# Hyperbolic loops of a four-layer graph network: the 65th coordinate's sums taken once per two row blocks

## The chip, the cores and the metric

The kernel runs on one core of one Trainium2 chip. The metric is device time of a run in microseconds (us). TensorE is PE in the profile, VectorE DVE, ScalarE ACT, GpSimd POOL; SP's queue issues nearly all DMAs.

## What is computed

Four layers run over 3327 nodes with 64 features each, padded to 3328 = 26 blocks of 128; every layer adds to x what it computes from a normalised x and the 0/1 adjacency matrix. Layers 0 and 3 are the hyperbolic ones:

```python
h = relu(layernorm(x))
x_tan = logmap0(h)
adj_att = sigmoid(left + right.T) * adj         # left, right: x_tan times a vector
x_local = logmap(h[:, None, :], h[None, :, :])  # hyperbolic log between every two nodes
support = einsum('ij,ijd->id', adj_att, x_local)
x = x + proj(expmap(h, support))
```

Layer 1 sums neighbours with weights that halve along a row, layer 2 is a signed attention with two gated cells; both need only the adjacency matrix and x. Layer 3 is layer 0 with other constants and a curvature.

## The kernel before, in words

**The form of a hyperbolic layer.** The log between two nodes is a factor, which depends on an inner product of 65 coordinates, times a combination of both points. So a layer needs a weight for each pair of nodes (sigmoid times adjacency times an arctangent of the inner product plus a constant) and then the sum over nodes of weight times the node's 65 coordinates. Coordinates 1 to 64 are in Xr, the 65th (x0) in X0.

**Tiles.** `hyperbolic_series` holds the 3328 output nodes in two halves of 13 blocks; its chunks take 4, 3, 3 and 3 blocks of each half, so that one tile is 128 source nodes by 2 x 512 or 2 x 384 output nodes. For each chunk it goes over the 26 row blocks of source nodes: K = 104 tiles, numbered k, in the order chunk, then row block b. Two row blocks that follow each other (2j and 2j + 1) are a pair.

**One tile's way.**
- `load` (L368) brings the adjacency tile by a DMA of SP's queue, in layer 0 only; layer 3 finds it in SBUF as fp8 masks, which layer 1 made.
- `sigmoid` (L568) writes `sig` on ScalarE; L570 multiplies the adjacency into it on GpSimd.
- `products` (L581, L582) makes the inner products on TensorE, two fp16 matmuls for each half, into a PSUM slot.
- `angle` (L587) takes the arctangent in place on ScalarE.
- `weights` (L591) adds PC and multiplies by `sig` on VectorE, the result into `sig`; then the slot is free.
- `sums` (L600) multiplies Xr of the row block with `sig`, 64 output rows for each half, in fp32. After every second row block L608 does the same for the 65th coordinate: X0 is 32 columns wide, only its first is not zero, and the four operands (two row blocks, two halves) stand side by side in the array's four column groups, 32 output rows each. So a pair has one such group of matmuls, and `to_m2` (L639) adds the rows of the two row blocks later.

Four PSUM slots serve all this. One is the accumulator of the running chunk; three go round for products.

**The order.** The program in the loops is written by hand: under `manual_schedule` ScalarE, VectorE, TensorE and GpSimd run their instructions as written, each in its order. Step j issues sums of tiles 2j - 2 and 2j - 1, products of 2j + 3 and 2j + 4, weights of 2j and 2j + 1, arctangents of 2j + 2 and 2j + 3, sigmoids of 2j + 3 and 2j + 4. At the end of a chunk `out_of` (L618, ScalarE) takes the sums out, `back` (L627) transposes them, and `to_m`, `to_m2` (L633 to L643, VectorE, with copies on ScalarE) reduce them. SP's DMAs stand in an order that the tile framework chooses from when their buffers are free. In layer 0 GpSimd also makes `diag` (L560), two operations for each chunk.

**Ahead of the loops** the points are normalised and split in fp16 parts: Xp and Xe hold the parts that TensorE transposes, LT a row vector of `left`, which a DMA (L534) writes to memory so that later chunks read it back as `leftB` (L388). The first tile's sigmoid stands behind the last preparation on VectorE (L537). **After layer 0** come some 15 us of small VectorE operations, and then layer 1, whose loads (L1289, 832 KB each, seven buffers) and masks (L1317) need nothing of layer 0's result.

Of the kernel before, what the change touches and what calls it, by code (L numbers as in the profile page):

```python
# [19 lines left out]
P = 128  # L20
T = 26
NP = T * P
D = 64
# [6 lines left out]
PA, PB, PC, PF = 0.8235022297, 1.4, 1.7857925668, 1.1972493614  # L30
# [16 lines left out]
def tile_gnn4(ctx: ExitStack, tc: tile.TileContext, x, adjT, att0, b0, w1, bias1, w_gat, a_gat,  # L47
# [4 lines left out]
    V, G, A, PE = nc.vector, nc.gpsimd, nc.scalar, nc.tensor  # L52
# [268 lines left out]
    def hyperbolic_series(r, params, ok, masks=None, done=None):  # L321
# [17 lines left out]
        W = 512  # L339
        with ExitStack() as st:  # L340
            pers = st.enter_context(tc.tile_pool(name="hs", bufs=1))
            Xr = pers.tile([P, T, D], F32, name="Xr")
            X0 = pers.tile([P, T, 32], F32, name="X0")
            x2 = pers.tile([P, T], F32, name="x2")
            ia = pers.tile([P, T], F32, name="ia")
            XT = pers.tile([P, NP], F16, name="XT")

            XE = pers.tile([KE + 9, NP], F16, name="XE")
            Xp = pers.tile([P, T, 2 * D + 9], F16, name="Xp")
            hi, lo, F = Xp[:, :, :D], Xp[:, :, D:2 * D], Xp[:, :, 2 * D:]  # L350
            LT = pers.tile([T, P], F32, name="LT")
            right = pers.tile([P, T], F32, name="right")
            M = pers.tile([P, T, D], F32, name="M")
            M0, hm, mm = [pers.tile([P, T], F32, name=n) for n in ("M0", "hm", "mm")]
# [4 lines left out]
            px = st.enter_context(tc.tile_pool(name="hsx", bufs=2))  # L359
            small = {n: pers.tile([P, T], F32, name=n) for n in ("rr", "k", "kb", "bx", "bk", "bh")}  # L360
            adjs = {}
            tiles = [(c, b) for c in chunks for b in range(T)]
            K = len(tiles)

            def load(k):
                c, b = tiles[k]
                adjs[k] = px.tile([P, 2, W], F32, name="adj", bufs=4)[:, :, :c[1] * P]
                nc.sync.dma_start(adjs[k], halves(adjT[b * P:(b + 1) * P, :], c))  # L368

            XC, XF, leftB = {}, {}, {}  # L370
# [1 line left out]
            def halves(t, c):  # L372

                return t.rearrange("p (o i) -> p o i", o=2)[:, :, c[0] * P:(c[0] + c[1]) * P]
# [14 lines left out]
                                                        ap=[[0, P], [HT * P, 2], [1, n]]))  # L389

            if masks is None:
                for k in range(4):
                    load(k)
            with tc.tile_pool(name="hsp", bufs=1) as tp, tc.tile_pool(name="hsps", bufs=2, space=PSUM) as ps, \
                    tc.manual_schedule(engines={mybir.EngineType.Activation, mybir.EngineType.DVE,
                                                mybir.EngineType.PE, mybir.EngineType.Pool}):
                H, R, sq, sr = [tp.tile([P, T, D], F32, name=n) for n in ("H", "R", "sq", "sr")]
                Xe = tp.tile([P, T, KE + 9], F16, name="Xe")
                E, Fe = Xe[:, :, D:KE], Xe[:, :, KE:]
                G.memset(X0, 0.0)  # L400
                G.memset(E[:, :, 6:], SX)
# [4 lines left out]
                def new(name):  # L406
                    return tp.tile([P, T], F32, name=name)
# [40 lines left out]
                x0, x0s, rest, z, lr, left, good = [new(n) for n in ("x0", "x0s", "rest", "z", "lr2", "left", "good")]  # L448
# [83 lines left out]
                PE.transpose(junk[:T, :P], left, ident)  # L532
                V.tensor_copy(LT, junk[:T, :P])
                nc.sync.dma_start(left_row, LT)  # L534
                V.tensor_copy(X0[:, :, 0], x0)
                V.scalar_tensor_tensor(good, x2, X2_MIN, nodes, op0=OP.is_ge, op1=OP.mult)
                V.reduce_sum(ok, good, axis=AX.X)  # L537

# [4 lines left out]
            with tc.tile_pool(name="hsw", bufs=2) as wk, tc.tile_pool(name="hsps", bufs=1, space=PSUM) as ps, \  # L543
                    tc.manual_schedule(engines={mybir.EngineType.Activation, mybir.EngineType.DVE,
                                                mybir.EngineType.PE, mybir.EngineType.Pool}):
                acc, sigs, Ls, later = {}, {}, {}, {}
                slots = [ps.tile([P, 2, W], F32, name=f"slot{k}") for k in range(4)]
                made = [0]

# [14 lines left out]
                def sigmoid(k):  # L564

                    c, b = tiles[k]
                    sig = sigs[k] = new("sig", c, bufs=7)
                    A.activation(sig, leftB[c], AF.Sigmoid, bias=right[:, b:b + 1])  # L568
                    adj = adjs.pop(k) if masks is None else halves(masks[b // 2][:, b % 2, :], c)
                    G.tensor_tensor(sig, adj, sig, op=OP.mult)  # L570

                def products(to):

# [10 lines left out]
                def angle(k):  # L584

                    L = Ls[k][:, :, :tiles[k][0][1] * P]
                    A.activation(L, L, AF.Arctan, scale=PA / SX ** 2)  # L587

                def weights(k):
                    slot, sig = Ls.pop(k), sigs[k]  # L590
                    V.scalar_tensor_tensor(sig, slot[:, :, :tiles[k][0][1] * P], PC, sig, op0=OP.add, op1=OP.mult)  # L591
                    slots.append(slot)

                def sums(k):
                    c, b = tiles[k]
                    n = c[1] * P
                    if b == 0:
                        acc[c] = slots.pop(0)
                    for o in range(2):
                        PE.matmul(acc[c][o * D:(o + 1) * D, 0, :n], Xr[:, b, :], sigs[k][:, o, :],  # L600
                                  start=b == 0, stop=b == T - 1)
                    if b % 2 == 1:

                        for i in range(2):
                            w = sigs.pop(k - 1 + i)
                            for o in range(2):
                                q = 32 * (2 * i + o)
                                PE.matmul(acc[c][q:q + 32, 1, :n], X0[:, b - 1 + i, :], w[:, o, :],  # L608
                                          start=b == 1, stop=b == T - 1, tile_position=(0, q))
                    if b == T - 1:  # L610
                        a = new("sum", c, bufs=1)
                        j = (k + 1) // 2
                        later[j, 1] = lambda: out_of(c, a, 0)
                        later[j + 1, 0] = lambda: out_of(c, a, 1)
                        later[j + 2, 0] = lambda: back(j + 2, c, a)

                def out_of(c, a, o):
                    A.activation(a[:, o, :], acc[c][:, o, :c[1] * P], AF.Copy)  # L618
                    if o == 1:
                        slots.append(acc.pop(c))  # L620
# [8 lines left out]

                def to_m(j, c, slot):  # L630
                    pm = slot[:, 0, :c[1] * P].rearrange("p (t o d) -> p o t d", o=2, d=D)
                    prod = wk.tile([P, 2, 2, 4, D], F32, name="prod", bufs=1)[:, :, :, :c[1], :]
                    V.tensor_mul(prod[:, 0], by_tiles(Xr, c), pm)  # L633
                    A.activation(prod[:, 1], pm, AF.Square)
                    later[j + 1, 0] = lambda: to_m2(j + 1, c, slot, pm, prod)
# [12 lines left out]

                sigmoid(0)
                for j in range(-1, K // 2 + 5):  # L650
                    for k in (2 * j - 2, 2 * j - 1):
                        if 0 <= k < K:
                            sums(k)
                    for i in range(2):
                        k = 2 * j + i
                        products(2 * j + 3 + i)
                        if 0 <= k < K:
                            weights(k)
                        if i == 0 and (j, 0) in later:
                            later.pop((j, 0))()  # L660
                        products(2 * j + 4)
                        if k + 2 < K:
                            angle(k + 2)
                        if k + 3 < K:
                            if masks is None and k + 5 < K:
                                load(k + 5)
                            sigmoid(k + 3)
                        if i == 1 and (j, 1) in later:
                            later.pop((j, 1))()
                    if at(2 * j + 10, 1):  # L670
                        columns(at(2 * j + 10, 1))
# [7 lines left out]
            with tc.tile_pool(name="hse", bufs=1) as tp:  # L679
# [14 lines left out]
                w = mul("w", mm, bk2)  # L694
# [9 lines left out]
                th, t, a1, d, y2 = [new(n) for n in ("th", "t", "a1", "d", "y2")]  # L704
# [1016 lines left out]
```

## Time and profile before

| what | us |
|---|---|
| median of three runs | 782.72 |
| lowest and highest | 781.93, 782.87 |
| the profiled execution | 785.62 |
| its span | 783.4 |
| layer 0's loop, first to last VectorE weight | 39.8 to 251.8 |
| layer 3's loop, the same | 548.5 to 756.2 |
| TensorE, VectorE, ScalarE, GpSimd busy | 643.9, 508.4, 564.2, 423.5 |

The span is the time between the first and the last instruction of the profiled execution, and the sums are made against it. In the page's slices each digit is the busy share of a fortieth of the span, in tenths. In the groups of instructions a row gives line, engine, operation, the tiles written and read with their shapes, how often it ran, then busy time and the mean of one in ns, and after the bar the idle time just ahead of it and what ended that. A timeline row gives start and duration; rows that follow each other without a break are merged, with a count.

### The profile page before, as it was taken

Reading aid. Unit: us, or ns where it says so; the run is one execution under the profiler, and the core shown is the slowest. Engines: PE = TensorE matmul, PEld = TensorE weight load, DVE = VectorE, ACT = ScalarE, POOL = GpSimd, SP = SyncE. Lnnn points to the kernel's source line nnn. Section 1 sums busy time; section 2 is a strip of 40 time slices with the busy share of each in tenths; the row PEclk is TensorE's granted clock in tenths of the full one; section 3 lists DMA queues with packets and bytes.
Section 4 is the critical chain, followed back from the end, with each engine's and each line's share of the span. In section 5 each row is a group of like instructions: output and inputs, shape, how many; then the busy total and the mean of one; then the engine's idle time right before and its main releaser. Section 6 shows DMA issues by size and latency. Waiting matters only on the chain. (4 is left out here: it accounts for less than half of the span.)

```text
span 783.4 us, 11543 instructions
## 1 busy us (share of the span) xinstructions
PE 643.9 (82%) x4199; PEld 261.3 (33%) x4199; DVE 508.4 (65%) x752; ACT 564.2 (72%) x733; POOL 423.5 (54%) x324
## 2 busy tenths in 40 slices
PE   0789999999999049999996598717899999999970
PEld 0622233333333014444443364215222333333320
DVE  6545555555554879997995794996555555555456
ACT  2678888888886357776776266625888888888863
POOL 3399999999997040001230000004888788788840
PEclk9999999999999559998998799956999999999995
DMA  3889877777774028997954380001000001000001
GB/s 62 293 242 307 257 225 199 229 219 210 204 203 135 0 88 295 376 374 270 340 222 174 114 281 1 1 0 44 9 0 14 23 1 37 2 1 1 1 1 49
DMA packets 57620, 107.82 MB, mean 138 GB/s; under 512 B 8753, under 2 KB 33489, under 8 KB 57553
## 3 DMA queue, kind: packets, MB, share of 16 engines
q1 hardware_dynamic: 53200, 106.97, 42.6%
q10 hardware_dynamic: 4352, 0.02, 0.3%
q8 instruction: 35, 0.57, 0.3%
q14 instruction: 33, 0.26, 0.1%
HBM read 103.72 MB, written 0.88 MB: 134 GB/s over the span
## 5 line engine op out<-in xcount | busy, mean ns | idle before, releaser
L591 DVE SCALAR_TENSOR_TENSOR sig<-slot,sig 128x768 f32<-128x768 f32 (+1 forms) x208 | 212.9, 1023 | 196.8 <-POOL sig L570 192.3
L587 ACT ACTIVATE slot<-slot 128x768 f32<-128x768 f32 (+1 forms) x208 | 177.2, 852 | 57.7 <-PE slot L582 57.4
L570 POOL TENSOR_TENSOR sig<-adj,sig 128x768 f32<-128x768 f32 (+1 forms) x104 | 201.0, 1957 | 18.2 <-ACT sig L568 16.0
L568 ACT ACTIVATE sig<-leftB,right 128x768 f32<-128x768 f32 (+1 forms) x208 | 203.1, 976 | 2.3 <-DVE ok L537 2.3
L570 POOL TENSOR_TENSOR sig<-mask,sig 128x768 f32<-128x768 fp8e4 (+1 forms) x104 | 173.1, 1677 | 45.8 <-ACT sig L568 45.8
L600 PE MATMUL slot<-sig,Xr 128*64 128x384 f32 (+1 forms) x832 | 170.9, 529 | 7.5 <-DVE sig L591 7.4
L581 PE MATMUL slot<-XC,XT 128*128 128x384 f16 (+1 forms) x416 | 143.2, 344 | 7.8 <-DVE sig L591 2.5
L582 PE MATMUL slot<-XF,XE 73*128 73x384 f16 (+1 forms) x416 | 142.4, 342 | 0.0
L1330 ACT ACTIVATE w<-cnt,ebias 128x832 bf16<-128x832 f32 x104 | 94.0, 950 | 41.9 <-PE cnt L1324 41.9
L1239 DVE TENSOR_SCALAR_CACHE_REDUCE same<-adj 128x1664 bf16<-128x1664 f32 x52 | 97.6, 1878 | 0.3
L608 PE MATMUL slot<-sig,X 128*32 128x384 f32 (+1 forms) x832 | 94.9, 528 | 0.0
L600 PEld LDWEIGHTS slot<-sig,Xr 128*64 128x64 f32 x832 | 49.6, 136 | 89.8 <-issue 61.5
L1324 PE MATMUL cnt<-mask,after 128*128 128x416 fp8e4 x208 | 56.6, 356 | 22.9 <-DVE mask L1317 20.0
L581 PEld LDWEIGHTS <-XT 128*128 128x128 f16 x416 | 40.8, 98 | 97.7 <-issue 69.8
L190 POOL TENSOR_TENSOR mask<-mask,offdiag 128x128 fp8e4<-128x128 fp8e4 x26 | 15.0, 593 | 106.1 <-PE cnt L1324 106.1
L400 POOL MEMSET X<- 128x832 f32 x2 | 1.6, 791 | 107.7 <-PE pt L1225 107.7
L1341 PE MATMUL acc<-w,h 128*64 128x416 bf16 x416 | 49.2, 360 | 9.9 <-ACT h L182 9.4
L1324 PE MATMUL cnt<-mask,rest 128*128 128x416 fp8e4 x208 | 56.1, 353 | 0.3 <-ACT w L1330 0.3
L1317 DVE TENSOR_SCALAR mask<-adj 128x1664 fp8e4<-128x1664 f32 x52 | 52.6, 1029 | 0.0
L582 PEld LDWEIGHTS <-XE 73*128 73x128 f16 x416 | 40.9, 98 | 32.4 <-issue 8.7
L608 PEld LDWEIGHTS slot<-sig,X 128*32 128x32 f32 x832 | 16.4, 108 | 68.5 <-issue 68.5
L1539 PE MATMUL bank<-mask,h 128*64 128x416 fp8e4 x416 | 39.1, 347 | 0.0
(300 smaller groups left out, 515.6 us busy)
## 6 DMA issues: line engine op xcount, KB each, us to landing
adj<-in SPq DMA_DIRECT2D x65, 832.0 KB, 6.1
adj<-in SPq DMA_DIRECT2D x78, 384.0 KB, 4.1
adj<-in SPq DMA_DIRECT2D x27, 512.0 KB, 5.1
leftB<-left SPq DMA_DIRECT2D x6, 384.0 KB, 3.6
XC<-XT SPq DMA_DIRECT2D x12, 96.0 KB, 3.9
X<-in SPq DMA_DIRECT2D x2, 416.0 KB
out<-X SPq DMA_DIRECT2D x2, 416.0 KB
XF<-XT SPq DMA_DIRECT2D x6, 96.0 KB, 4.3
```

The costliest lines, as they stand in the source:

```text
L568: A.activation(sig, leftB[c], AF.Sigmoid, bias=right[:, b:b + 1])
L570: G.tensor_tensor(sig, adj, sig, op=OP.mult)
L581: PE.matmul(L[:, o, :c[1] * P], XT[:, rows], XC[c][:, o, :], start=True, stop=False)
L582: PE.matmul(L[:, o, :c[1] * P], XE[:KE, rows], XF[c][:, o, :], start=False, stop=True)
L587: A.activation(L, L, AF.Arctan, scale=PA / SX ** 2)
L591: V.scalar_tensor_tensor(sig, slot[:, :, :tiles[k][0][1] * P], PC, sig, op0=OP.add, op1=OP.mult)
L600: PE.matmul(acc[c][o * D:(o + 1) * D, 0, :n], Xr[:, b, :], sigs[k][:, o, :], start=b == 0, stop=b == T - 1)
L608: PE.matmul(acc[c][q:q + 32, 1, :n], X0[:, b - 1 + i, :], w[:, o, :], start=b == 1, stop=b == T - 1, tile_position=(0, q))
L1239: V.tensor_scalar(same, adj, 0.0, 0.0, op0=OP.is_equal, op1=OP.add, accum_out=count)
L1317: V.tensor_scalar(mask, adj, 1.0, None, op0=OP.is_equal, saturate=False)
L1324: PE.matmul(cnt[o][:, h, :BK], w, cols(k, o, h), start=w is after and steps[k][1] == T - 1, stop=True, skip_group_check=True)
L1330: A.activation(ws[k][:, o, :, :], cnt[o][:, :, :BK], AF.Exp, scale=-LN2, bias=ebias)
```

## The change

The weights of an even row block are scaled by the ratio of the two blocks' 65th coordinates, row by row, so that the pair's weights can be added to one tile and multiplied by one X0, that of the odd block. As `sig` of an even block then carries that ratio, its sums for coordinates 1 to 64 use Xs, which is Xr times the inverse ratio.

- `weights` has a second VectorE operation for every even row block: the first writes (slot + PC) x sig back into the PSUM slot, the second multiplies by ratio and adjacency into `sig`. In layer 0 every second odd block, too, gets its adjacency on VectorE, by a second operation. GpSimd multiplies the adjacency into the other odd blocks only.
- `add` on GpSimd adds the two tiles of a pair to `pre`; `sums_of_pair` then puts two pairs (four row blocks) in one group of the 32-column matmuls. The thirteenth pair of a chunk isn't added: `sums` takes its two tiles directly.
- Ahead of the loops: one reciprocal and two multiplications on VectorE, Xs on GpSimd (832 elements a row). X0 is half as long.
- Buffers: eight adjacency tiles instead of four, nine `sig` instead of seven, three `pre`; `sum` and `prod` share one. Xp and LT lie in the pool of the preparation, whose space the loop's tiles take over.

The order of instructions of the changed kernel shows two more things. The first sigmoid of each layer waits for LT's DMA as well, as its tile covers LT. The first of layer 1's loads waits for VectorE's last reduction of layer 0's loop, as its buffer covers tiles of that loop, and the other six stand behind it in SP's queue; before, seven were issued between 20 us and the first half of layer 0's loop.

```diff
-            X0 = pers.tile([P, T, 32], F32, name="X0")
+            X0 = pers.tile([P, T // 2, 32], F32, name="X0")
+            Xs = pers.tile([P, T // 2, D], F32, name="Xs")
+            ratio, back_ratio = [pers.tile([P, T // 2], F32, name=n) for n in ("ratio", "back_ratio")]
-            Xp = pers.tile([P, T, 2 * D + 9], F16, name="Xp")
-            LT = pers.tile([T, P], F32, name="LT")
...
+            LEAD = 4
-                adjs[k] = px.tile([P, 2, W], F32, name="adj", bufs=4)[:, :, :c[1] * P]
+                adjs[k] = px.tile([P, 2, W], F32, name="adj", bufs=LEAD + 4)[:, :, :c[1] * P]
...
+                Xp = tp.tile([P, T, 2 * D + 9], F16, name="Xp")
+                LT = tp.tile([T, P], F32, name="LT")
...
-                V.tensor_copy(X0[:, :, 0], x0)
+                pair = x0.rearrange("p (t s) -> p t s", s=2)
+                V.tensor_copy(X0[:, :, 0], pair[:, :, 1])
+                V.reciprocal(rest, x0)
+                inverse = rest.rearrange("p (t s) -> p t s", s=2)
+                V.tensor_mul(back_ratio, pair[:, :, 1], inverse[:, :, 0])
+                V.tensor_mul(ratio, pair[:, :, 0], inverse[:, :, 1])
+                G.tensor_tensor(Xs, Xr.rearrange("p (t s) d -> p t s d", s=2)[:, :, 0, :],
+                                back_ratio[:, :, None].to_broadcast([P, T // 2, D]), op=OP.mult)
...
-                    sig = sigs[k] = new("sig", c, bufs=7)
+                    sig = sigs[k] = new("sig", c, bufs=9)
                     A.activation(sig, leftB[c], AF.Sigmoid, bias=right[:, b:b + 1])
-                    adj = adjs.pop(k) if masks is None else halves(masks[b // 2][:, b % 2, :], c)
-                    G.tensor_tensor(sig, adj, sig, op=OP.mult)
+                    given[k] = adjs.pop(k) if masks is None else halves(masks[b // 2][:, b % 2, :], c)
+                    if b % (2 if masks is not None else 4) == 1:
+                        G.tensor_tensor(sig, given.pop(k), sig, op=OP.mult)
...
-                    V.scalar_tensor_tensor(sig, slot[:, :, :tiles[k][0][1] * P], PC, sig, op0=OP.add, op1=OP.mult)
+                    c, b = tiles[k]
+                    L = slot[:, :, :c[1] * P]
+                    mask = given.pop(k, None)
+                    V.scalar_tensor_tensor(sig if mask is None else L, L, PC, sig, op0=OP.add, op1=OP.mult)
+                    if b % 2 == 0:
+                        V.scalar_tensor_tensor(sig, L, ratio[:, b // 2:b // 2 + 1], mask, op0=OP.mult, op1=OP.mult)
+                    elif mask is not None:
+                        V.tensor_mul(sig, L, mask)
                     slots.append(slot)
+
+                def add(p):
+                    c, b = tiles[2 * p]
+                    if b // 2 < PAIRS - 1:
+                        pres[p] = new("pre", c, bufs=3)
+                        G.tensor_tensor(pres[p], sigs[2 * p], sigs[2 * p + 1], op=OP.add)
+
+                def zeroth(c, w, first, last):
+                    for i, (t, src) in enumerate(w):
+                        for o in range(2):
+                            r = 32 * (2 * i + o)
+                            PE.matmul(acc[c][r:r + 32, 1, :c[1] * P], X0[:, t, :], src[:, o, :],
+                                      start=first, stop=last, tile_position=(0, r))
+
+                def sums_of_pair(p):
...
+                    if t % 2 == 1:
+                        zeroth(c, [(t - 1, pres.pop(p - 1)), (t, pres.pop(p))], t == 1, False)
...
-                        PE.matmul(acc[c][o * D:(o + 1) * D, 0, :n], Xr[:, b, :], sigs[k][:, o, :],
-                                  start=b == 0, stop=b == T - 1)
-                    if b % 2 == 1:
-
-                        for i in range(2):
-                            w = sigs.pop(k - 1 + i)
-                            for o in range(2):
-                                q = 32 * (2 * i + o)
-                                PE.matmul(acc[c][q:q + 32, 1, :n], X0[:, b - 1 + i, :], w[:, o, :],
-                                          start=b == 1, stop=b == T - 1, tile_position=(0, q))
+                        PE.matmul(acc[c][o * D:(o + 1) * D, 0, :n], Xr[:, b, :] if b % 2 else Xs[:, b // 2, :],
+                                  sigs[k][:, o, :], start=b == 0, stop=b == T - 1)
...
                     if b == T - 1:
-                        a = new("sum", c, bufs=1)
+                        zeroth(c, [(b // 2, sigs.pop(k - 1 + i)) for i in range(2)], False, True)
...
                 for j in range(-1, K // 2 + 5):
+                    if 0 <= j - 1 < K // 2:
+                        add(j - 1)
+                    sums_of_pair(j - 2)
                     for k in (2 * j - 2, 2 * j - 1):
...
-                            if masks is None and k + 5 < K:
-                                load(k + 5)
+                            if masks is None and k + 2 + LEAD < K:
+                                load(k + 2 + LEAD)
```

More of the change, by code (lines that the diff above doesn't have):

```diff
@@ L348, in hyperbolic_series @@
             XE = pers.tile([KE + 9, NP], F16, name="XE")
-            Xp = pers.tile([P, T, 2 * D + 9], F16, name="Xp")
-            hi, lo, F = Xp[:, :, :D], Xp[:, :, D:2 * D], Xp[:, :, 2 * D:]
-            LT = pers.tile([T, P], F32, name="LT")
             right = pers.tile([P, T], F32, name="right")
@@ L391, in hyperbolic_series @@
             if masks is None:
-                for k in range(4):
+                for k in range(LEAD):
                     load(k)
@@ L397, in hyperbolic_series @@
                 H, R, sq, sr = [tp.tile([P, T, D], F32, name=n) for n in ("H", "R", "sq", "sr")]
+                Xp = tp.tile([P, T, 2 * D + 9], F16, name="Xp")
+                hi, lo, F = Xp[:, :, :D], Xp[:, :, D:2 * D], Xp[:, :, 2 * D:]
+                LT = tp.tile([T, P], F32, name="LT")
                 Xe = tp.tile([P, T, KE + 9], F16, name="Xe")
@@ L545, in hyperbolic_series @@
                                                 mybir.EngineType.PE, mybir.EngineType.Pool}):
-                acc, sigs, Ls, later = {}, {}, {}, {}
+                acc, sigs, Ls, later, given, pres = {}, {}, {}, {}, {}, {}
+                PAIRS = T // 2
                 slots = [ps.tile([P, 2, W], F32, name=f"slot{k}") for k in range(4)]
@@ L590, in weights @@
                     slot, sig = Ls.pop(k), sigs[k]
-                    V.scalar_tensor_tensor(sig, slot[:, :, :tiles[k][0][1] * P], PC, sig, op0=OP.add, op1=OP.mult)
-                    slots.append(slot)
+                    c, b = tiles[k]
[6 more added lines that the diff above has]
+                        V.tensor_mul(sig, L, mask)
+                    slots.append(slot)
+                def add(p):
[10 more added lines that the diff above has]
+                def sums_of_pair(p):
+                    if not 0 <= p < K // 2:
+                        return
+                    c, b = tiles[2 * p]
+                    t = b // 2
+                    if t % 2 == 1:
+                        zeroth(c, [(t - 1, pres.pop(p - 1)), (t, pres.pop(p))], t == 1, False)
                 def sums(k):
@@ L599, in sums @@
                     for o in range(2):
-                        PE.matmul(acc[c][o * D:(o + 1) * D, 0, :n], Xr[:, b, :], sigs[k][:, o, :],
-                                  start=b == 0, stop=b == T - 1)
-                    if b % 2 == 1:
-                        for i in range(2):
-                            w = sigs.pop(k - 1 + i)
-                            for o in range(2):
-                                q = 32 * (2 * i + o)
-                                PE.matmul(acc[c][q:q + 32, 1, :n], X0[:, b - 1 + i, :], w[:, o, :],
-                                          start=b == 1, stop=b == T - 1, tile_position=(0, q))
+                        PE.matmul(acc[c][o * D:(o + 1) * D, 0, :n], Xr[:, b, :] if b % 2 else Xs[:, b // 2, :],
+                                  sigs[k][:, o, :], start=b == 0, stop=b == T - 1)
+                    if b < T - 2:
+                        del sigs[k]
                     if b == T - 1:
-                        a = new("sum", c, bufs=1)
+                        zeroth(c, [(b // 2, sigs.pop(k - 1 + i)) for i in range(2)], False, True)
+                        a = wk.tile([P, 2, 2, 4, D], F32, name="sum", bufs=1)
+                        a = a.rearrange("p o s t d -> p o (s t d)")[:, :, :n]
                         j = (k + 1) // 2
@@ L631, in to_m @@
                     pm = slot[:, 0, :c[1] * P].rearrange("p (t o d) -> p o t d", o=2, d=D)
-                    prod = wk.tile([P, 2, 2, 4, D], F32, name="prod", bufs=1)[:, :, :, :c[1], :]
+                    prod = wk.tile([P, 2, 2, 4, D], F32, name="sum", bufs=1)[:, :, :, :c[1], :]
                     V.tensor_mul(prod[:, 0], by_tiles(Xr, c), pm)
```

## The prediction

> **What bounds the kernel now.** I began with the page's busy slices, to find the two stretches that hold the changed loops. In the stretches 60 to 250 and 560 to 755 us (busy time by engine) TensorE is busy 185.89 of 190 and 193.57 of 195 us.
>
> ```profile
> PE   0789999999999049999996598717899999999970
> DVE  6545555555554879997995794996555555555456
> ACT  2678888888886357776776266625888888888863
> POOL 3399999999997040001230000004888788788840
> PEclk9999999999999559998998799956999999999995
> ```
>
> Both loops fill TensorE at full clock; GpSimd is full in the first only, VectorE about half busy. Matmul ends are modelled, so I took the beat from starts in the timeline. A steady stretch of the layer-3 loop (first column start, second duration, in us):
>
> ```profile
> 629.26 1.51 PE L600 MATMUL slot<-sig,Xr 128*64 128x384 f32 x8
> 630.71 0.85 PE L608 MATMUL slot<-sig,X 128*32 128x384 f32 x8
> 631.49 0.34 PE L581 MATMUL slot<-XC,XT 128*128 128x384 f16 x1
> 632.91 0.20 PEld L600 LDWEIGHTS slot<-sig,Xr 128*64 128x64 f32 x4 [0.32 <-issue]
> ```
>
> For one pair of row blocks at 384 columns: sums 1.44, 65th coordinate 0.79, products 1.42, together 3.65 us with no real gap. At 512 columns the starts 557.12, 558.98, 559.98 and 561.83 give 1.87, 1.00 and 1.85: 4.72. In layer 0 the same view shows GpSimd with no pause at all:
>
> ```profile
> 138.24 16.41 POOL L570 TENSOR_TENSOR sig<-adj,sig 128x768 f32<-128x768 f32 x9
> ```
>
> 16.41/9 = 1.823, so 3.65 per pair: TensorE and GpSimd are both full there. The groups, shapes kept apart, price the rest (busy, mean ns | idle before):
>
> ```profile
> L591 DVE SCALAR_TENSOR_TENSOR sig<-slot,sig 128x768 f32<-128x768 f32 x156 | 149.2, 956 | 129.3 <-POOL sig L570 127.7 <-ACT slot L587 1.6
> L570 POOL TENSOR_TENSOR sig<-mask,sig 128x768 f32<-128x768 fp8e4 x78 | 121.2, 1562 | 26.4 <-ACT sig L568 26.4
> L591 DVE SCALAR_TENSOR_TENSOR sig<-slot,sig 128x1024 f32<-128x1024 f32 x52 | 63.7, 1224 | 67.6 <-POOL sig L570 64.6 <-ACT slot L587 2.9
> L570 POOL TENSOR_TENSOR sig<-adj,sig 128x1024 f32<-128x1024 f32 x26 | 60.6, 2363 | 13.1 <-ACT sig L568 12.2 <-ACT slot L587 1.0
> ```
>
> VectorE's 192 us of waiting for GpSimd is room, not loss. The chain that ended last agrees: through layer 3 it steps from one sums group to the next, and only at chunk ends over ScalarE.
>
> ```profile
> 636.63 1.44 PE slot L600 x8
> 640.27 1.44 PE slot L600 x8
> ```
>
> [...] The 956 ns holds beside a full GpSimd, and the new operations too read one operand from PSUM[...]; no VectorE row here writes PSUM. ScalarE's PSUM-to-PSUM arctangent (799 ns) isn't dearer than its SBUF sigmoid (923).
>
> **The change, for four row blocks (two pairs).**
>
> TensorE loses one of two 65th-coordinate groups. 384 columns: 2 x (1.44 + 1.42) + 0.79 = 6.51 instead of 7.30. 512: 2 x (1.87 + 1.85) + 1.00 = 8.44 instead of 9.44. A chunk has six such fours; its thirteenth pair keeps its own group.
>
> VectorE goes from 4 operations to 7 in layer 0 (a second one for each even block and for every other odd one) and 6 in layer 3. Between starts I take duration - 0.09 if the next doesn't depend, duration + 0.03 if it does (small operations at 764.20 and 766.22 show 0.22 and 0.10 for 0.19), and 0.05 for the pointer scalar (0.24 against 0.18 in the small rows). The PSUM-writing operation is unseen: from below a little cheaper than 956 (as ScalarE's is), from above the read and the write of 768 elements one after the other, +0.80. I take 956[...]. Even block 0.99 + 0.92 = 1.91, odd masked here 0.99 + 0.87 = 1.86, odd plain 0.87. Layer 0: 2 x 1.91 + 1.86 + 0.87 = 6.55; layer 3: 5.56. At 512 columns 8.40 and 7.15.
>
> GpSimd, layer 0: one mask and two additions (same operand types as the mask) instead of four masks, 3 x 1.82 = 5.47 instead of 7.29. Layer 3: two fp8 masks and two additions, 2 x 1.56 + 2 x 1.82 = 6.77 instead of 6.22; at 512 columns 2 x 2.02 + 2 x 2.36 = 8.77.
>
> ScalarE is untouched: starts 1.55 apart per block, 6.2 per four.
>
> So the beat is set in layer 0 by VectorE and TensorE level, in layer 3 by GpSimd just above TensorE. Do the PSUM slots allow it? A slot is now free only after the second VectorE operation: 1.95 there, 0.87 from product to arctangent, 0.85 for that, 3.7 of the 4.9 that three slots give at 1.63 a block (before, 2.7 of 5.5). The 1.2 left must take TensorE's sums[...] (1.44, or 2.23 with the group). Following the waits by hand over eight blocks of layer 0, a slot comes back up to 0.05 late, as products stand behind the sums in any case, and an addition ends 0.1 after TensorE would use it: I take 6.6, and 8.5 at 512 columns. Layer 3: 6.77 and 8.77.
>
> Gain, layer 0: 3 chunks x 6 x (7.30 - 6.60) = 12.6; first chunk 6 x (4 x 2.33 - 8.5) = 4.9, and its two diagonal operations of 1.04, which now stop a full GpSimd, 2.1. Layer 3: 18 x (7.30 - 6.77) = 9.5, 6 x (9.44 - 8.77) = 4.0. Sum 33.1.
>
> **The starts.** LT moves into a pool whose space the loops' tiles reuse; in the changed order the first sigmoid of each layer waits for the landing of LT's DMA. Now it waits for VectorE only:
>
> ```profile
> 34.91 1.28 ACT L568 ACT_TABLE_LOAD   x1 [2.62 <-DVE ok L537]
> 35.53 0.52 SPq L534 DMA_DIRECT2D left<-LT  x1
> ...
> 544.91 0.48 SPq L534 DMA_DIRECT2D left<-LT  x1
> 546.42 0.38 SPq L388 DMA_DIRECT2D leftB<-left  x1
> ```
>
> The last row waits for that landing, so it takes about 1.5. In layer 0 LT's DMA can issue behind the XF issue that ends at 34.75, landing 36.3, so sigmoids start 1.4 later; in layer 3 546.4 instead of 545.16, 1.3 later. Queued behind are all of ScalarE's loop, then VectorE and TensorE. Block 0 no longer needs a GpSimd mask, but block 1 does: sums of block 1 start some 0.9 and 1.2 later. Three small VectorE operations (0.7) hide under that DMA, and GpSimd's Xs (832 elements, about 2 us) ends before block 1's sigmoid; without that cover, 2.
>
> **Moved past.** SP's order changes: seven layer-1 loads of 832 KB, now issued during layer 0, wait for VectorE's last reduction of the loop (257.3 now). Seven at 375 GB/s (rate at 322 to 342 us) are 16 us; the first is needed 15 us later (272.68), and the third mask only at 290.31. Cost nothing while that tail covers them; without it, up to 16. Adjacency tiles are held longer, but there are eight buffers instead of four. At 6.6 per four layer 0 asks 393 KB x 4/6.6 = 238 GB/s; 234 took a DMA share of 0.80 (140 to 160 us), so loads stay hidden.
>
> **Chunk ends.** A chunk of 26 blocks takes 49.9 (152.82 to 202.74) against 13 x 3.65 = 47.4. There ScalarE (about 2 us of copies) and VectorE (1.8) have less room than before: six boundaries at 0.5 each, 3.0.
>
> Total: 33.1 - 2.1 - 3.0 = 28. The profiled execution took 785.62 with a span of 783.4; it becomes 757.6. It lies 2.9 above the median of 782.72, so the median becomes 754.7; say 755.
>
> **Rivals.** (a) VectorE's PSUM writes cost 0.25 more. Layer 0's four then takes 6.55 + 3 x 0.25 = 7.30, no gain there; layer 3 (6.06) keeps its own: 755 + 19.6 = 775. For: nothing prices it, and VectorE is level with TensorE.[...] (b) Slower: a PSUM write doubles the operation (+0.80, 1.07 at 512 columns). Layer 0's four is 8.95 and 11.6, losing 18 x 1.65 + 6 x 2.3 = 43 instead of gaining 20; layer 3 7.16 and 9.29, gaining 3: about 783 - 3 + 43 + 5 = 828. It decides from 0.35: at 0.25 the net gain is 8, and each 0.1 beyond costs 24 x 0.3 = 7. (c) A fuller VectorE slows GpSimd by a tenth[...]. Layer 3's four becomes 7.45 and 9.65, losing 4 instead of gaining 13.5; layer 0's additions fit: 773.[...] (d) Better: no loss at boundaries or starts and TensorE alone sets the beat: 18 x 0.79 + 6 x 1.00 per layer, 40, so 743.
>
> **Chances.** Forecast with its neighbours down to (d) 0.63, (a) 0.12, (c) 0.09, slower like (b), from its threshold up, 0.12, and 0.04 that gains and losses cancel. A measurement of this kernel can tell about 0.2% (1.6 us) from no change. Faster 0.84, same 0.04, slower 0.12. The range runs from 745, near (d), to 780, above (a) and (c); outside lie mainly the slower cases.
>
> **What would show it.** Sums groups of TensorE should start on average 3.3 apart in layer 0 and 3.4 in layer 3 (384 columns), and the 32-column group once per two pairs. The PSUM-writing VectorE group should read about 956 ns: above 1200 it is (a), above 1300 (b). GpSimd's additions should read 1.82; 2.0 is (c). The first sigmoids should wait for a DMA. Were VectorE waiting for loads in layer 1, the moved loads would be what I got wrong.

## The result, and the profile after

The changed kernel takes 834.49 us (833.58 to 835.75, four runs), the kernel before beside it 782.80: a ratio of 1.066 with a 95% interval of 1.0642 to 1.0681. The forecast was 755 (745 to 780). The profiled execution took 833.58 with a span of 831.8, 48.4 more than the span before. From the start of a loop's first weight operation on VectorE to that of its last, the two loops grew by 23.2 us (211.0 to 234.2) and 19.9 (206.8 to 226.7), and the way from there to VectorE's multiplication behind the loop's last sums (`to_m`) by 3.9 and 2.3 (4.2 before, 8.1 and 6.5 after): 49.3 together, so the loss is in the two loops and at their ends.

The busy slices of the changed kernel's page:

```profile
PE   0698888889888327998995698527998898998960
DVE  6588768787788579997996794996776776777656
ACT  3677777786786255777776287346776887788752
POOL 3366675765666120001230000033886787787740
PEclk9889999999999757999998799758999999999995
```

TensorE's unbroken row of nines is gone: in layer 0's loop it has eights but for two slices, in layer 3's nines and eights, and no other engine has nines in their place. From 60 to 250 us TensorE is busy 166.47 of 190 us, VectorE 151.32, ScalarE 145.99, GpSimd 123.45; from 580 to 795 us 195.09 of 215, 155.75, 168.91 and 168.96. The granted clock is 1.00 in both stretches, as before, and layer 3, whose loop loads no adjacency, lost nearly as much as layer 0, so neither the clock nor the loads explain the loss. Nor did any instruction become dearer than was priced (groups, shapes kept apart):

```profile
L618 POOL TENSOR_TENSOR pre<-sig 128x768 f32<-128x768 f32 x72 | 130.3, 1818 | 0.0
L606 DVE SCALAR_TENSOR_TENSOR slot<-slot,sig 128x768 f32<-128x768 f32 x96 | 92.2, 960 | 43.6 <-ACT slot L599 43.6
L608 DVE SCALAR_TENSOR_TENSOR sig<-slot,ratio,mask 128x768 f32<-128x768 f32 x39 | 39.7, 1018 | 1.4
```

What changed stands in the view of waits (who waits for whom: total us, how often, the longest; PEld is TensorE's loading of weights). Before, then after:

```profile
POOL sig L570 <- ACT sig L568: 61.7, 56, 12.2
ACT slot L587 <- PE slot L582: 57.4, 93, 2.1
```

```profile
POOL sig L582 <- ACT sig L579: 139.3, 54, 5.4
ACT slot L599 <- PE slot L594: 100.6, 53, 4.7
PEld slot L624 <- POOL pre L618: 67.7, 47, 3.2
```

Two of the waits were there and about doubled; the third is new, as the 32-column group did not read a result of GpSimd's before. Read as a sentence: GpSimd waits for ScalarE, ScalarE for TensorE, TensorE for GpSimd. That is a circle, and it can be walked in the timeline of layer 0 (start, duration, in brackets the idle time ahead and what ended it):

```profile
139.50 0.84 PE L624 MATMUL slot<-pre,X 128*32 128x384 f32 x4 [0.87 <-POOL pre L618]
140.27 0.87 PE L642 MATMUL slot<-sig,Xs 128*64 128x384 f32 x4
...
141.71 0.34 PE L593 MATMUL slot<-XC,XT 128*128 128x384 f16 x1
...
142.58 0.80 ACT L599 ACTIVATE slot<-slot 128x768 f32<-128x768 f32 x1 [2.15 <-PE slot L594]
...
143.29 0.93 ACT L579 ACTIVATE sig<-leftB,right 128x768 f32<-128x768 f32 x1
...
144.29 1.81 POOL L582 TENSOR_TENSOR sig<-adj,sig 128x768 f32<-128x768 f32 x1 [3.06 <-ACT sig L579]
...
146.07 3.60 POOL L618 TENSOR_TENSOR pre<-sig 128x768 f32<-128x768 f32 x2
...
147.94 0.84 PE L624 MATMUL slot<-pre,X 128*32 128x384 f32 x4 [0.87 <-POOL pre L618]
```

TensorE's 32-column group waits for an addition (139.50). Behind it in TensorE's order stand two sums (140.27) and the products (141.71); the arctangent waits for these (142.58); the next sigmoid needs nothing from them, but stands behind that arctangent on ScalarE (143.29); GpSimd's mask waits for the sigmoid (144.29), the addition stands behind the mask (146.07), and the next group waits for the addition (147.94). The stretches between these starts are 0.77, 1.44, 0.87, 0.71, 1.00, 1.78 and 1.87, in sum 8.44 us for four row blocks, where VectorE, the fullest engine, has 6.55 of work by the prediction's sum. That a place in the order holds an instruction back shows in the sigmoid: in experiment 1, where it stands ahead of the arctangent, ScalarE waits 3.6 us in all ahead of its 208 sigmoids, all of it for LT's DMA, so here at 143.29 it had only its place in the order to wait for. In the chain that ended last (the work that the end of the execution waited for, followed back step by step) GpSimd has 19%, by its masks (10%) and additions (9%); before, the chain went over TensorE's sums.

**A correction.** The section on the order says that step j issues the products of tiles 2j + 3 and 2j + 4. That is wrong: `products(to)` makes the tiles below `to`, so step j makes 2j + 2 and 2j + 3. The arctangent of 2j + 2 in step j therefore waits for products of the same step, made after group and sums. With the lead stated there it would not.

### The profile page after: what moved, and what is told of

It reads as the page before. It is cut to its first block, busy times and chain, and to the rows that moved or that the text cites. A ratio compares the mean times of both kernels' runs of the same rounds, so it can differ in the third digit from the quotient of the medians.

```text
span 831.8 us, 10633 instructions
## 1 busy us (share of the span) xinstructions
PE 643.2 (77%) x3815; PEld 256.6 (31%) x3815; DVE 640.9 (77%) x886; ACT 561.2 (67%) x733; POOL 376.0 (45%) x294
## 5 line engine op out<-in xcount | busy, mean ns | idle before, releaser
L599 ACT ACTIVATE slot<-slot 128x768 f32<-128x768 f32 (+1 forms) x208 | 176.9, 850 | 101.1 <-PE slot L594 100.6
L618 POOL TENSOR_TENSOR pre<-sig 128x768 f32<-128x768 f32 (+1 forms) x96 | 186.8, 1954 | 0.0
L606 DVE SCALAR_TENSOR_TENSOR slot<-slot,sig 128x768 f32<-128x768 f32 (+1 forms) x128 | 131.4, 1027 | 67.5 <-ACT slot L599 67.5
L606 DVE SCALAR_TENSOR_TENSOR sig<-slot,sig 128x768 f32<-128x768 f32 (+1 forms) x80 | 81.9, 1024 | 42.4 <-POOL sig L582 41.5
L582 POOL TENSOR_TENSOR sig<-mask,sig 128x768 f32<-128x768 fp8e4 (+1 forms) x52 | 87.1, 1675 | 52.4 <-ACT sig L579 52.4
L624 PE MATMUL slot<-pre,X 128*32 128x384 f32 (+1 forms) x384 | 80.1, 526 | 35.1 <-POOL pre L618 35.1
L642 PE MATMUL slot<-sig,Xs 128*64 128x384 f32 (+1 forms) x416 | 97.9, 550 | 8.2 <-issue 8.2
L582 POOL TENSOR_TENSOR sig<-adj,sig 128x768 f32<-128x768 f32 (+1 forms) x28 | 54.7, 1952 | 86.9 <-ACT sig L579 86.9
L642 PE MATMUL slot<-sig,Xr 128*64 128x384 f32 (+1 forms) x416 | 93.0, 526 | 0.7 <-DVE sig L610 0.6
L608 DVE SCALAR_TENSOR_TENSOR sig<-slot,ratio,mask 128x768 f32<-128x768 f32 (+1 forms) x52 | 56.4, 1085 | 1.8
L608 DVE SCALAR_TENSOR_TENSOR sig<-slot,ratio,adj 128x768 f32<-128x768 f32 (+1 forms) x52 | 56.4, 1085 | 1.8
```

What stands on the lines that cost most here:

```text
L582: G.tensor_tensor(sig, given.pop(k), sig, op=OP.mult)
L606: V.scalar_tensor_tensor(sig if mask is None else L, L, PC, sig, op0=OP.add, op1=OP.mult)
L608: V.scalar_tensor_tensor(sig, L, ratio[:, b // 2:b // 2 + 1], mask, op0=OP.mult, op1=OP.mult)
L618: G.tensor_tensor(pres[p], sigs[2 * p], sigs[2 * p + 1], op=OP.add)
L642: PE.matmul(acc[c][o * D:(o + 1) * D, 0, :n], Xr[:, b, :] if b % 2 else Xs[:, b // 2, :], sigs[k][:, o, :], start=b == 0, stop=b == T - 1)
```

## The experiments

Two theories, both named in what was expected. LOOP: the circle above takes the time, and anything that opens it gives the time back. SLOTS: a PSUM slot is held longer, by the second VectorE operation, and its way round sets the pace. A "four" below is the time for four row blocks in the steady part of a chunk, from VectorE's starts; the table is for all runs. The ratios further down are to the kernel before, run beside each experiment.

| kernel | layer 0: 512 / 384 | layer 3: 512 / 384 | median us |
|---|---|---|---|
| before | 9.32 / 7.30 | 9.43 / 7.29 | 782.80 |
| the forecast | 8.5 / 6.6 | 8.77 / 6.77 | 755 |
| changed | 10.81 / 8.44 | 10.46 / 8.18 | 834.49 |
| 1 sigmoid first | 8.67 / 6.74 to 6.89 | 8.55 / 6.74 | 762.44 |
| 2 group later | 8.57 / 6.74 | 8.63 / 6.74 | 778.04 |
| 3 both | 8.57 / 6.74 | 8.55 / 6.74 | 760.35 |
| 4 no GpSimd mask in layer 0 | 9.82 / 7.69 | 10.46 / 8.18 | 816.89 |
| 5 before, sigmoid first | 9.32 / 7.29 | 9.43 / 7.29 | 775.83 |
| 6 dose | 13.45 / 9.23 | 11.48 / 8.98 | 892.62 |
| 7 both, dose | 8.56 / 6.74 | 9.62 / 7.0 to 7.4 | 778.74 |
| 8 LT kept | 10.80 / 8.43 | 10.47 / 8.18 | 831.52 |
| 9 products earlier | 8.45 / 6.58 | 8.61 / 6.60 | 767.12 |
| 10 both, LT kept | 8.57 / 6.74 | 8.56 / 6.74 | 757.67 |
| 11 as 10, fewer masks | 8.57 / 6.74 | 8.57 / 6.74 | 757.45 |
| 12 sigmoid first, products earlier, LT kept | 8.45 / 6.58 | 7.9 to 8.4 / 6.2 to 6.5 | 748.50 |

**1. The sigmoid ahead of the arctangent.**

```diff
-                        if k + 2 < K:
-                            angle(k + 2)
                         if k + 3 < K:
...
                             sigmoid(k + 3)
+                        if k + 2 < K:
+                            angle(k + 2)
```

> The changed kernel with one swap of order: on ScalarE the sigmoid of tile k+3 stands ahead of the arctangent of tile k+2. Same work, same buffers. Theory LOOP (a circle of waits through four in-order engines sets the beat: sums, product, arctangent, sigmoid behind it, GpSimd's mask behind that, its addition behind the mask, the 32-column group behind the addition, sums again; 8.44 us per four row blocks in layer 0): the sigmoid no longer waits for TensorE, the circle is cut, a four at 384 columns falls from 8.44 to about 6.8 in both layers, the median to about 766 (755 to 782), below the kernel before. Theory SLOTS (a PSUM slot is held for a second VectorE operation, and products come one tile later than I had assumed): nothing changes, 830 to 836.

Measured: 762.44 us, ratio 0.972 (0.9671 to 0.977). No work was taken away; two neighbours on ScalarE changed places, 72 us went, and with them GpSimd's 19% of the chain that ended last (the page's line):

```profile
PE 22%; DVE 14%; ACT 6%; issue 3%; POOL 1%; DMA 0%; ACTq 0%; DVEq 0%; POOLq 0%
```

**2. The 32-column group behind the step's first products**, and **3. both orders.**

```diff
-                    sums_of_pair(j - 2)
+                    last = (j - 2) % PAIRS == PAIRS - 2
+                    if last:
+                        sums_of_pair(j - 2)
...
+                        if i == 0 and not last:
+                            sums_of_pair(j - 2)
```

> The changed kernel with the 32-column group of a four put behind the step's products on TensorE instead of ahead of its sums (the sixth four of a chunk stays where it was, so that the accumulator is complete in time). LOOP: TensorE's next products no longer wait for GpSimd's addition; the circle now goes over two fours instead of one (about 11.3 us for two), below what the engines need, so a four falls to about 6.9 and the median to about 770 (758 to 788). SLOTS: 830 to 836, perhaps slower, as a slot's product still waits for the second VectorE operation.

> Both re-orderings together. LOOP: no more than the better of the two, about 765 (753 to 782), since each alone already cuts the circle and the rest is set by VectorE (6.55 per four in layer 0) and GpSimd (6.77 in layer 3). SLOTS: 830 to 836.

Measured: 778.04, ratio 0.9936 (0.9898 to 0.9974), and 760.35, ratio 0.9698 (0.9648 to 0.9748). In 2 the circle is opened on TensorE instead of ScalarE, in 3 on both. In 2 the steady fours fall to 6.74 as forecast, but where a later chunk begins, the fours from its third and from its seventh block stay at 7.7 to 8.5 (7.6 to 8.5 in the changed kernel), so it lies at the slow end of what was expected. With the circle open another one is the next limit, the chain of experiment 3 in layer 3:

```profile
617.64 0.98 DVE slot L606
...
618.64 1.03 DVE sig L608
...
620.53 0.78 PE slot L624 x8
621.31 1.44 PE slot L642 x8
...
623.55 0.80 ACT slot L599
...
624.38 0.98 DVE slot L606
```

This is the way round of a slot: two VectorE operations, products, group, sums, products, arctangent, 6.74 from 617.64 to 624.38. So SLOTS is real, at 6.74, and not what made 8.44.

**4. No mask on GpSimd in layer 0**; VectorE masks those blocks too.

```diff
-                    if b % (2 if masks is not None else 4) == 1:
+                    if masks is not None and b % 2 == 1:
```

> The changed kernel, but in layer 0 VectorE multiplies the adjacency into every odd row block, so GpSimd only adds there. Layer 3 is as in the changed kernel. LOOP: the addition no longer stands behind a mask that waits for a sigmoid, so layer 0 is freed although VectorE has eight operations per four instead of seven (two even at 1.91, two odd at 1.86: 7.54); a four of layer 0 falls from 8.44 to about 7.6, the median to about 815 (808 to 822), all of it in layer 0. SLOTS: every slot is now held for two VectorE operations, so layer 0 gets slower: 838 to 850.

Measured: 816.89, ratio 1.0415 (1.0361 to 1.047). VectorE, which in SLOTS is the pinched engine, got more work in layer 0, and its four fell from 8.44 to 7.69; layer 3, untouched, stayed at 8.18. GpSimd's mask is a link of the circle.

**5. A control: the order of experiment 1 in the kernel before.**

> The kernel before with the order of experiment 1: in each step the next sigmoid is issued ahead of the arctangent. LOOP (the lost time of the changed kernel is a circle of waits that the addition on GpSimd closed): the kernel before has no such circle, its loops are held by TensorE (185.9 busy of 190 us), so the order is worth 0 to 3 us there: 780 to 783. ORDER (the exchange is better in any kernel, and says nothing of the change): some 20 us or more come off here too, 755 to 763.

Measured: 775.83, ratio 0.9933 (0.991 to 0.9956). More than the 0 to 3 us that LOOP allowed: the steady fours don't move (TensorE is busy all of 590 to 740 us), but the tiles where a chunk begins do (in layer 0 the four from a later chunk's seventh block takes 7.6 in place of 8.4), in the profiled execution 10 us over both loops. The medians are 5.9 us apart (781.75 beside it). If the order is worth as much in the changed kernel, some 6 of the 72 us of experiment 1 come from it and the rest from the circle; that split was not measured by itself. With that order in both, the change is a gain: 0.972 against 0.9933, intervals apart.

**6 and 7. A dose of 0.73 us on GpSimd ahead of every second pair's addition**, in the changed kernel and in that of experiment 3.

```diff
                         pres[p] = new("pre", c, bufs=3)
+                        if b // 2 % 2 == 1:
+                            G.memset(pres[p], 0.0)
```

> The changed kernel with a fill of the sum's tile on GpSimd, some 0.75 us at 768 elements and 0.95 at 1024, ahead of the addition of every second pair; it changes no value. GpSimd is idle 35% of layer 0's loop and 22% of layer 3's. LOOP: GpSimd's path is inside the circle, so each dose lengthens a four by itself: about 36 x 0.75 + 12 x 0.95 = 38 us, 872 (864 to 882). SLOTS, and any reason that lies on other engines: the dose falls in idle time, 834 to 840.

> The same dose in the kernel of experiment 3 (both orders changed), which took 760. LOOP: the circle is open there, so layer 0, where GpSimd works about 5.5 us of a four of 6.8, hides the dose (0 to 3 us), and layer 3, where GpSimd is full at 6.74 of a four, pays it: 18 x 0.75 + 6 x 0.95 = 19 us; together 780 (774 to 786). If the dose costs the same in both layers as in the changed kernel, about 798, the circle was not opened by the orders.

Measured: 892.62, ratio 1.1421 (1.1369 to 1.1474), and 778.74, ratio 0.9967 (0.995 to 0.9985). In 6 an engine that idled a third of the time passes the whole dose on: GpSimd's mask comes 9.23 after the one before (the timeline of experiment 6), not 8.44.

```profile
142.35 1.81 POOL L582 TENSOR_TENSOR sig<-adj,sig 128x768 f32<-128x768 f32 x1 [3.06 <-ACT sig L579]
144.11 0.73 POOL L619 MEMSET pre<- 128x768 f32 x1
...
151.58 1.81 POOL L582 TENSOR_TENSOR sig<-adj,sig 128x768 f32<-128x768 f32 x1 [3.07 <-ACT sig L579]
```

At 384 columns that is +0.79 in either layer, at 512 in layer 3 +1.02. The total of 58, not 38, is taken up at the end. In 7 layer 0's loop grew by 0.4 us and layer 3's, where GpSimd is full, by 16.2: with the circle open the dose costs only where there is no room for it.

**8. LT's tile kept through the layer.**

```diff
+            LT = pers.tile([T, P], F32, name="LT")
...
-                LT = tp.tile([T, P], F32, name="LT")
```

> The changed kernel with the tile LT (512 bytes of a partition) put back among those that live through the layer, so that the loop's first tiles don't take its memory while its DMA is under way. If the first sigmoid of each layer waits for that DMA because of the memory, as the trace has it (3.62 us in layer 3), the starts come back: 1.4 and 1.3 us, 831.8 (830 to 833). If something else is as late as the DMA, nothing: 834.5.

Measured: 831.52, ratio 1.0648 (1.0622 to 1.0673); the interval overlaps that of the changed kernel, so the times alone don't settle it, but the timelines do. The first sigmoid of layer 3 in the changed kernel, then in this one:

```profile
571.18 1.15 ACT L579 ACTIVATE sig<-leftB,right 128x1024 f32<-128x1024 f32 x1 [3.62 <-DMA left<-LT]
```

```profile
565.91 1.15 ACT L579 ACTIVATE sig<-leftB,right 128x1024 f32<-128x1024 f32 x1 [2.77 <-DVE ok L547]
```

From the copy into LT to the first sigmoid it was 2.12 (569.06 to 571.18) and is 1.28; in layer 0 4.46 and 2.56. Together 2.7 us were the DMA's.

**9. The products of tile 2j + 4 at the end of step j**, which is the order stated ahead of the prediction.

```diff
-                        products(2 * j + 4)
+                        products(2 * j + 4 + (i == 1 and 2 * j % T >= 6))
```

> The changed kernel with the products of tile 2j+4 made at the end of step j, one tile earlier than it does, from the fourth step of each chunk on; this is the order that the prediction's steps followed by mistake. LOOP: the arctangent of the next step then waits for no product that stands behind the group on TensorE, the circle opens as it does in experiment 1, and a four at 384 columns comes to some 6.8 to 7.1 us in place of 8.44 and 8.18: 762 to 772, say 767. If the order of the products isn't the step that failed, a four stays over 8 us and the time at 830 to 836.

Measured: 767.12, ratio 0.978 (0.9754 to 0.9806). The fours are now those of the prediction, 6.58 and 8.45 in layer 0 where it had 6.6 and 8.5. The 32-column group comes once in 6.57 us (timeline of TensorE, layer 0):

```profile
174.28 0.85 PE L624 MATMUL slot<-pre,X 128*32 128x384 f32 x8
...
180.85 0.85 PE L624 MATMUL slot<-pre,X 128*32 128x384 f32 x8
```

The time is 12 above 755. The start of a chunk keeps the old order there, and its fours are long: up to 10.8 in the first chunk, and in layer 0's others 8.2 to 9.6 from the third and the seventh block, where experiment 1 has 7.3 to 7.9. Experiment 12, which has both orders, is below 755.

**10 and 11. Experiment 3 with LT kept; then GpSimd's masks in layer 3 as few as in layer 0.**

```diff
-                    if b % (2 if masks is not None else 4) == 1:
+                    if b % 4 == 1:
```

> Experiment 3 (both orders) with the tile LT kept through the layer as in experiment 8, which took 3 us off: 757.4 (755 to 760). If the loop's start is no longer what is late when the circle is open, 760.

> As the run before, and in layer 3 too GpSimd masks every fourth row block and not every second; VectorE masks the other odd ones with one more operation each. A four of layer 3 took 6.74 us at 384 columns in experiment 3, as in layer 0, where GpSimd is not full. If the circle through the four PSUM tiles (two operations of VectorE, products, group, sums, arctangent) holds both layers, nothing: 757 (755 to 760). If GpSimd, full in layer 3, holds it there, a four falls to some 6.5: 24 x 0.25 = 6 us, 751.

Measured: 757.67, ratio 0.9679 (0.9658 to 0.97), and 757.45, ratio 0.9669 (0.9648 to 0.969). Relieving GpSimd in layer 3 does nothing: there, too, the slots' way round holds a four at 6.74.

**12. Sigmoid first, products one tile earlier, LT kept.**

> The sigmoid ahead of the arctangent (experiment 1), the products one tile earlier (experiment 9) and LT kept (experiment 8), the group where the changed kernel has it. Experiment 9 has the shortest fours inside a chunk (6.58 at 384 columns, TensorE's own work being 6.5) and slow ones where a chunk begins (9.6 and 8.4); experiment 1 has quick beginnings (7.86, 7.85) and fours of 6.75 to 6.9. If TensorE alone holds the inside once its products are early, both gains add: 762.4 - 3 - 18 x 2 x 0.2 = 752 (749 to 757). If the circle through the PSUM slots comes back with the sigmoid ahead of the arctangent, fours stay at 6.74 and the time at 757 to 760.

Measured: 748.50, ratio 0.9573 (0.9539 to 0.9608): faster than both kernels, and than the best end of what was expected. Its chain in layer 3 is TensorE from group to group, 6.51 us:

```profile
600.97 0.78 PE slot L624 x8
...
607.48 0.78 PE slot L624 x8
```

6.51 is what the prediction worked out as TensorE's work for a four.

## Why the prediction was wrong

**The step that failed** is "Following the waits by hand over eight blocks of layer 0, a slot comes back up to 0.05 late ... and an addition ends 0.1 after TensorE would use it: I take 6.6". The walk itself isn't written out, but the order that stands ahead of it has the products one tile earlier than the program does. With that lead the arctangent that the next sigmoid and mask stand behind doesn't wait for products that stand behind the group, and no circle closes; experiment 9 makes that order from each chunk's fourth step on and has the forecast's fours. In the order as written, the same instructions take 8.44 and 8.18. With the circle open by other means, the way round of the slots in that order takes 6.74 (experiments 3 and 11), a little above the 6.6 that was set. For layer 3 and for 512 columns the prediction did not even walk: it took the fullest engine's work (6.77, 8.77) for the beat.

Point by point:

- **Prices: right.** The write to PSUM cost 960 ns where 956, the price of a row that writes to SBUF, was taken as an estimate, the pointer scalar 0.06 where 0.05, an addition 1.818 where 1.82, and GpSimd was not slowed (1818 ns for an addition, 1821 for a mask before). Rivals (a), (b) and (c) all hung on these prices (the 0.25 of (a) and the tenth of (c) were the author's assumptions), and none happened; nor did (d), as the beat was far from TensorE's alone. (b)'s 828 is near the measured 834.5 by accident: its mechanism, a PSUM write of 1.75 us (956 ns and 768 x (1224 - 956)/256 more, from the rows of 768 and 1024 elements), is refuted.
- **The sum over fours: wrong in sign.** In place of 33.1 gained (30.1 with the chunk ends), the loops lost 43.1, and the loops' ends, for which nothing was set, 6.2: there, too, the last group waits 2.50 us (layer 0) and 2.25 us (layer 3) for an addition and stands ahead of the last sums.
- **Starts: the wait was right, its size in part by luck.** The sigmoids were to start 2.7 us later, of which 2.1 went into the sum; experiment 8 finds 2.7, split otherwise (1.9 and 0.8 where 1.4 and 1.3 were set). And layer 0's first weight operation was not later at all (39.31, 39.81 before): the copy into LT stood at 32.70, before at 34.15.
- **Layer 1's loads, moved behind VectorE's last reduction: right.** The first issues at 283.96 and the first masks start at 299.53; VectorE waits 0.4 us for loads.
- **Chunk ends.** Three us for six boundaries can't be separated from the circle; with it open (experiment 10), layer 0's third chunk of 13 pairs takes 46.5, and 13/2 fours of 6.74 are 43.8, so 2.7 remain where before there were 2.5 (49.9 against 47.4). The 0.5 more for each that was set doesn't show.
- **The signs named.** The sums groups came 4.22 and 4.09 us apart on average (half a four) where 3.3 and 3.4 were named; this one failed. The PSUM-writing group, the additions, layer 3's first sigmoid and VectorE's wait in layer 1 read as they were to.
- **The missing rival.** All four rivals were about an engine's work or a price. None was a new wait: the group, which had read VectorE's result, now waits for GpSimd, and the prediction's bound from full engines can't see that. What stands behind a waiting instruction was asked for the DMA at the start, and not for the group at the head of TensorE's step.

## What to carry to other kernels

When a step is handed to another engine, and the engines run in order as the rows from 139.50 to 147.94 us do, walk one period of the program as it is written, from the new wait through whatever stands behind it on each engine, and see whether the walk comes back to its own start; its length, divided by the number of periods that it spans, is a lower bound on the period even if no engine is full. Read off the first and last value that an index takes before trusting such a walk: one tile of lead was the difference between 6.6 and 8.4 us. In the profile, the circle showed as engines idle with each waiting for the next (139.3, 100.6 and 67.7 us), and it was told from a full engine by exchanging two independent instructions (72 us, and 5.9 with the same exchange in a kernel without the circle as a control), or by a small dose on an idle engine that came through whole (0.73 us in, 0.79 more for a four).

## What the runs showed beside

A VectorE operation that writes its result back to PSUM cost the same here as one that writes to SBUF, 960 against 957 ns at 768 elements and 1227 against 1225 at 1024. A scalar read from SBUF for each row added some 60 ns (1018 against 957).

Where the dose of experiment 6 cost most over its length, TensorE slowed down. The timeline in layer 0 at 512 columns:

```profile
63.90 1.05 PE L626 MATMUL slot<-pre,X 128*32 128x512 f32 x4
...
67.17 1.92 PE L626 MATMUL slot<-pre,X 128*32 128x512 f32 x4 [2.22 <-POOL pre L620]
69.03 1.84 PE L644 MATMUL slot<-sig,Xs 128*64 128x512 f32 x4
```

After a pause of 2.22 us (3.13 between weight loads) the same four matmuls take 1.92 in place of 1.05 us, and the sums that follow 1.84 in place of 1.08; those at 70.70 us take 1.02 again. In the changed kernel the pause at this place is 1.21 us and nothing slows. What the group and the sums took longer, 0.87 and 0.76 us, is what a four of 13.45 has over 10.81 and the dose's 1.0. It was not the only place: a matmul of the 512-column group takes 672 ns on average in experiment 6 and 605 in the changed kernel, one of the sums with Xs 763 and 650.

The page of experiment 6 has the granted clock at 8 tenths in the two slices from 66.8 to 111.3 us; in the changed kernel it is 1.00 between 60 and 120 us. The pause's length alone doesn't decide, though: at the ends of the changed kernel's loops one of 2.50 us was followed by a clock of 0.50 (275.9 to 279.1 us; sums of 1.55 in place of 0.87), and one of 2.25 was not (1.00 from 801 to 807). Over the whole profiled execution the mean granted clock is 0.913 of 890.7 us in experiment 6 and 0.922 of 831.8 in the changed kernel, so 77.5 and 64.9 us of clock were not granted: some 13 more, where experiment 6 missed its forecast by 20 (an estimate from these figures, not of the loops alone). That the pause is the cause was not tried by itself.
